# Layer 1's vertical 5-tap convolution: two rows at a time from eight products in place of ten

## The chip, the cores and the metric

The kernel runs on one core of a Trainium2 chip. The metric is device time in microseconds (us) for the whole kernel, the median of several runs; smaller is better. The kernel before takes 4054.06 us (three runs, 4048.38 to 4065.66).

## What is computed

Two layers work on an image tensor `x` of shape (2, 128, 256, 256): two images, 128 channels, 256 rows of 256 columns, all in float32. Layer 0 is an attention over windows of 8x8 pixels; the change does not touch it. Layer 1 is cut here to what matters:

```python
def _L1_conv_ref(x, w1, w3, w4):                    # x: after a group norm
    t1 = conv(x, w1, padding=((2, 2), (0, 0)))      # 5 taps along the rows, 128 -> 128 channels
    t3 = conv(t1, w3, padding=((1, 1), (0, 0)),     # 3 taps along the rows, each channel by itself
              feature_group_count=c)
    t2 = _unfold_w3_dil2(x)                         # columns w-2, w, w+2
    t4 = einsum('nckhw,ckg->nghw', t2, w4)          # 128 channels -> 8 groups
    t5 = t4[:, None] * t3.reshape(n, c // g, g, h, w)
    return t5.reshape(n, c, h, w)
...
x = x + _L1_conv_ref(_gn(x), w1, w3, w4)
```

With channels on the 128 partitions, each tap of `w1` is one 128x128 matrix that multiplies rows of `x`. Two rows of 256 columns are 512 elements, which fill one bank of the accumulator memory (PSUM). So a pair of output rows costs five products of a 128x128 matrix with 128x512 elements.

## The kernel before: the part of layer 1

The kernel walks through each image in 32 strips of 8 rows, so there are 64 strips in all. `xt` holds the 12 normalised rows that a strip needs, with two such buffers in turn. `t1` holds 10 rows: rows 0 and 1 are taken over from the strip before, rows 2 to 9 are new.

```python
rawp  = tile_pool("f_raw1", bufs=4); tp = tile_pool("f_t1", bufs=2); wk = tile_pool("f_wk1", bufs=2)
ps_pj = tile_pool("f_ps_pj1", bufs=1, space=PSUM)
ps_a  = tile_pool("f_ps_a", bufs=2, space=PSUM)     # 2 banks for the vertical convolution
ps_g  = tile_pool("f_ps_g", bufs=1, space=PSUM)
ps_b  = tile_pool("f_ps_b", bufs=1, space=PSUM)     # 4 tags, 4 banks
# ... cut: weights; xn = two buffers of [P, 12, 260] ...

def normalise1(b, s, k, mean, rstd):
    cur, prev = xn[k % 2], xn[(k + 1) % 2]
    # ... cut: the first strip of an image ...
        nc.gpsimd.tensor_copy(cur[:, 0:4, :], prev[:, 8:12, :])                       # L528
    n = 8 if s + 1 < NS else 5
    nc.vector.tensor_scalar(                                                          # L530
        cur[:, 4 : 4 + n, 2 : 2 + W], raws[b, s][:, 0:n, :], mean, rstd, ALU.subtract, ALU.mult)
    # ... cut ...

for k in range(NB * NS):
    b, s = divmod(k, NS)
    xt = xn[k % 2]
    t1 = tp.tile([P, 10, W], F32, tag="t1", name=f"t1_{k}")
    # ... cut: row 1 of the first strip of an image, three products over one row ...
        nc.gpsimd.tensor_copy(t1[:, 0:2, :], t1s[k - 1][:, 8:10, :])                  # L562
    # ... cut ...
    for j in (2, 4, 6, 8):
        n = 1 if j == 8 and s + 1 == NS else 2
        pa = ps_a.tile([P, 512], F32, tag="a", name=f"a_{k}_{j}")
        for tap in range(5):
            nc.tensor.matmul(                                                         # L570
                pa[:, : n * W], w1[:, tap, :], xt[:, j - 2 + tap : j - 2 + tap + n, 2 : 2 + W],
                start=tap == 0, stop=tap == 4)
        nc.scalar.copy(t1[:, j : j + n, :].rearrange("p r w -> p (r w)"), pa[:, : n * W])   # L574
    pg = ps_g.tile([P, 512], F32, tag="g", name=f"g_{k}")
    for tap in range(3):
        for j in range(4):
            nc.tensor.matmul(                                                         # L579
                pg[32 * j : 32 * j + 32, :], w4[:, tap, :],
                xt[:, 2 * j + 1 : 2 * j + 3, 2 * tap : 2 * tap + W], start=tap == 0, stop=tap == 2)
    t4 = wk.tile([P, 512], F32, tag="t4", name=f"t4_{k}")
    nc.scalar.copy(t4, pg)                                                            # L585
    t3 = wk.tile([P, 8, W], F32, tag="t3", name=f"t3_{k}")
    nc.scalar.activation(t3, t1[:, 0:8, :], AF.Copy, scale=w3[:, 0:1])                # L587
    for tap in (1, 2):
        nc.vector.scalar_tensor_tensor(                                               # L589
            t3, t1[:, tap : tap + 8, :], w3[:, tap : tap + 1], t3, ALU.mult, ALU.add)
    y = wk.tile([P, 8, W], F32, tag="y", name=f"y_{k}")
    for j in range(4):
        pb = ps_b.tile([P, 512], F32, tag=f"b{j}", name=f"b_{k}_{j}")
        nc.tensor.matmul(pb, sel[32 * j : 32 * j + 32, :], t4[32 * j : 32 * j + 32, :],
                         start=True, stop=True)                                       # L596
        nc.vector.tensor_tensor(y[...rows 2j, 2j+1...], pb, t3[...the same rows...], ALU.mult)   # L599
    nc.gpsimd.tensor_tensor(y[:, 0:3, :], y[:, 0:3, :], raws[b, s - 1][:, 5:8, :], ALU.add)   # L603
    nc.gpsimd.tensor_tensor(y[:, 3:8, :], y[:, 3:8, :], raws[b, s][:, 0:5, :], ALU.add)       # L604
    nc.gpsimd.dma_start(out[b, :, 8 * s : 8 * s + 8, :], y)                           # L605
    if k + 1 < NB * NS:
        start_strip(k + 1)        # loads rows, then normalise1
```

The order in which each engine gets its instructions isn't the order of this text: a scheduler ahead of the run sets it, from what it takes to be ready, and work of neighbouring strips is interleaved. On the chip each engine then follows its own list in that order.

Of the kernel before, what the change touches and what calls it, by code (L numbers as in the profile page):

```python
# [9 lines left out]
F32 = mybir.dt.float32  # L10
I32 = mybir.dt.int32
AF = mybir.ActivationFunctionType
ALU = mybir.AluOpType
# [5 lines left out]
P = 128  # L19
W = 256  # L20
# [458 lines left out]
def convolutions_fast(tc, io, x1_d, norm, st_y, out):  # L479

    nc = tc.nc
    NB, _, H, _ = io["x"].shape
    NS = H // 8
    with ExitStack() as l1:
        cst = l1.enter_context(tc.tile_pool(name="f_l1c", bufs=1))
        rawp = l1.enter_context(tc.tile_pool(name="f_raw1", bufs=4))
        tp = l1.enter_context(tc.tile_pool(name="f_t1", bufs=2))
        wk = l1.enter_context(tc.tile_pool(name="f_wk1", bufs=2))
        ps_pj = l1.enter_context(tc.tile_pool(name="f_ps_pj1", bufs=1, space=PSUM))
        ps_a = l1.enter_context(tc.tile_pool(name="f_ps_a", bufs=2, space=PSUM))  # L490
        ps_g = l1.enter_context(tc.tile_pool(name="f_ps_g", bufs=1, space=PSUM))
        ps_b = l1.enter_context(tc.tile_pool(name="f_ps_b", bufs=1, space=PSUM))

        w1 = cst.tile([P, 5, P], F32, tag="w1", name="w1")
        nc.sync.dma_start(w1, io["w1T"])
        w3 = cst.tile([P, 3], F32, tag="w3", name="w3")
        nc.sync.dma_start(w3, io["w3"])
        w4 = cst.tile([P, 3, 32], F32, tag="w4", name="w4")
        nc.sync.dma_start(w4, io["w4g"])
        sel = cst.tile([P, P], F32, tag="sel", name="sel")  # L500
        nc.sync.dma_start(sel, io["c_sel"])
        xn = [cst.tile([P, 12, 260], F32, tag=f"xm{i}", name=f"xm{i}") for i in range(2)]
        for i in range(2):
            nc.gpsimd.memset(xn[i], 0.0)

        raws = {}

        def load_rows1(b, s):

            if s == 0:  # L510
                pre = rawp.tile([P, 8, W], F32, tag="raw", name=f"raw1_{b}_pre")
                nc.sync.dma_start(pre[:, 5:8, :], x1_d[b][0][:, 0:3, :])
                raws[b, -1] = pre
            t = rawp.tile([P, 8, W], F32, tag="raw", name=f"raw1_{b}_{s}")
            nc.sync.dma_start(t[:, 0:5, :], x1_d[b][s][:, 3:8, :])
            if s + 1 < NS:
                nc.sync.dma_start(t[:, 5:8, :], x1_d[b][s + 1][:, 0:3, :])
            raws[b, s] = t

        def normalise1(b, s, k, mean, rstd):  # L520
            cur, prev = xn[k % 2], xn[(k + 1) % 2]
            if s == 0:
                nc.gpsimd.memset(cur[:, 0:1, :], 0.0)
                nc.vector.tensor_scalar(
                    cur[:, 1:4, 2 : 2 + W], raws[b, -1][:, 5:8, :], mean, rstd, ALU.subtract, ALU.mult
                )
            else:
# [3 lines that stand above are left out]
                cur[:, 4 : 4 + n, 2 : 2 + W], raws[b, s][:, 0:n, :], mean, rstd, ALU.subtract, ALU.mult  # L531
            )
            if n < 8:
                nc.gpsimd.memset(cur[:, 4 + n : 12, :], 0.0)

        norms = {}
        t1s = {}

        def start_strip(k):
            b, s = divmod(k, NS)  # L540
            if s == 0:
                norms[b] = norm.group(st_y[b], ps_pj, f"y{b}")
            load_rows1(b, s)
            normalise1(b, s, k, *norms[b])

        start_strip(0)
# [5 lines that stand above are left out]
            if s == 0:  # L552
                nc.gpsimd.memset(t1[:, 0:1, :], 0.0)
                pa = ps_a.tile([P, 512], F32, tag="a", name=f"a_{k}_first")
                for tap in (2, 3, 4):
                    nc.tensor.matmul(
                        pa[:, 0:W], w1[:, tap, :], xt[:, tap - 1, 2 : 2 + W],
                        start=tap == 2, stop=tap == 4,
                    )
                nc.scalar.copy(t1[:, 1, :], pa[:, 0:W])  # L560
            else:
                nc.gpsimd.tensor_copy(t1[:, 0:2, :], t1s[k - 1][:, 8:10, :])  # L562
            t1s[k] = t1
            if s + 1 == NS:
                nc.gpsimd.memset(t1[:, 9:10, :], 0.0)  # L565
            for j in (2, 4, 6, 8):
                n = 1 if j == 8 and s + 1 == NS else 2
                pa = ps_a.tile([P, 512], F32, tag="a", name=f"a_{k}_{j}")
                for tap in range(5):
                    nc.tensor.matmul(  # L570
                        pa[:, : n * W], w1[:, tap, :], xt[:, j - 2 + tap : j - 2 + tap + n, 2 : 2 + W],
                        start=tap == 0, stop=tap == 4,
                    )
                nc.scalar.copy(t1[:, j : j + n, :].rearrange("p r w -> p (r w)"), pa[:, : n * W])  # L574

            pg = ps_g.tile([P, 512], F32, tag="g", name=f"g_{k}")
            for tap in range(3):
# [3 lines that stand above are left out]
                        xt[:, 2 * j + 1 : 2 * j + 3, 2 * tap : 2 * tap + W],  # L581
                        start=tap == 0, stop=tap == 2,
# [7 lines that stand above are left out]
                    t3, t1[:, tap : tap + 8, :], w3[:, tap : tap + 1], t3, ALU.mult, ALU.add  # L590
# [6 lines that stand above are left out]
                    pb, sel[32 * j : 32 * j + 32, :], t4[32 * j : 32 * j + 32, :], start=True, stop=True  # L597
                )
                nc.vector.tensor_tensor(  # L599
                    y[:, 2 * j : 2 * j + 2, :].rearrange("p r w -> p (r w)"), pb,  # L600
                    t3[:, 2 * j : 2 * j + 2, :].rearrange("p r w -> p (r w)"), ALU.mult,
# [4 lines that stand above are left out]
            del raws[b, s - 1]  # L606
            if k + 1 < NB * NS:
                start_strip(k + 1)
# [592 lines left out]
```

## Time and profile before

| what | value |
|---|---|
| time, median of 3 runs | 4054.06 us |
| span of the profiled execution | 4070.9 us |
| TensorE matmuls, busy | 3641.6 us, 89% |
| VectorE, busy | 2272.4 us, 56% |
| ScalarE, busy | 1384.2 us, 34% |
| GpSimd, busy | 1084.9 us, 27% |
| last product of attention's stage begins | 2663.28 us |
| first products of layer 1 (`a_first`) begin | 2678.85 us |
| last products of layer 1 (`b`) begin | 4046.72 us |

In the profile's words PE is TensorE, DVE is VectorE, ACT is ScalarE, POOL is GpSimd; PEld is the loading of weights, which runs beside the matmuls. A group of instructions is named by its line in the kernel (the marks `L570` and so on in the code above), its engine, and what it writes and reads. "Busy" is the union of the instructions' durations; the mean of one matmul is longer than the pace at which matmuls follow each other, since they are pipelined. One float32 product in the program shows as two matmul instructions in the trace.

### The profile page before, as it was taken

What the parts mean: (1) busy time and instruction counts of PE and PEld (TensorE: products, weight loads), DVE (VectorE), ACT (ScalarE), POOL (GpSimd) and SP (SyncE); (2) the same over time, 40 slices, a digit from 0 to 9 for tenths busy, and PEclk for the clock granted to TensorE, in tenths of its full rate; (3) what the DMA queues carried; (4) which work ended last, traced back from release to release, by engine and by line L of the source; (5) the groups of instructions that cost most, each with busy time, mean ns of one, the idle gap of its engine ahead of it and who ended that gap; (6) DMA issues with size and microseconds to landing.
All of it is one profiled execution on the core that took longest, in us unless ns stands there. A gap on an engine that the chain in (4) does not pass through costs nothing. (4 is left out here: it accounts for less than half of the span.)

```text
span 4070.9 us, 144840 instructions
## 1 busy us (share of the span) xinstructions
PE 3641.6 (89%) x67638; PEld 2218.5 (54%) x67638; DVE 2272.4 (56%) x3377; ACT 1384.2 (34%) x2237; POOL 1084.9 (27%) x914
## 2 busy tenths in 40 slices
PE   0778988889989888988988989989999999999997
PEld 0556666666666666666666666643333334333333
DVE  8777656565655565656556565544444444444443
ACT  0333444444444444444444444422222222222221
POOL 1212222122222222212222122123333333333333
PEclk9999999999999999999999999989999999999998
DMA  9562212212212121221212211122222222222221
GB/s 377 190 198 81 68 60 68 68 55 68 72 56 65 55 68 55 73 68 55 68 55 73 68 55 65 34 92 104 97 90 104 104 93 96 101 103 104 90 97 70
DMA packets 71315, 362.10 MB, mean 89 GB/s; under 512 B 8496, under 2 KB 9136, under 8 KB 50224
## 3 DMA queue, kind: packets, MB, share of 16 engines
q1 hardware_dynamic: 43056, 218.49, 16.3%
q0 software_dynamic: 27648, 134.23, 8.4%
q8 instruction: 533, 8.73, 0.9%
q14 instruction: 78, 0.64, 0.1%
HBM read 218.48 MB, written 134.22 MB: 87 GB/s over the span
## 5 line engine op out<-in xcount | busy, mean ns | idle before, releaser
L570 PE MATMUL a<-xm,w 128*128 128x512 f32 (+1 forms) x2560 | 1129.8, 594 | 0.0
L570 PEld LDWEIGHTS a<-xm,w 128*128 128x128 f32 x2560 | 471.6, 188 | 654.5 <-issue 653.8
L589 DVE SCALAR_TENSOR_TENSOR t<-t,w,t 128x2048 f32<-128x2048 f32 x128 | 323.2, 2525 | 752.7 <-ACT t L574 752.6
L348 DVE COPY f_vt<-f_pv 64x512 f32<-64x512 f32 x512 | 354.1, 694 | 656.1 <-ACT f_vt L348 653.6
L348 ACT COPY f_vt<-f_pv 64x512 f32<-64x512 f32 x512 | 298.5, 583 | 756.2 <-PE f_pv L341 756.2
L341 PE MATMUL f_pv<-f_wqkvT,f_xn 128*64 128x128 f32 x8192 | 521.0, 286 | 29.6 <-issue 29.2
L374 PEld LDWEIGHTS f_s<-f_q,f_kt 32*64 32x64 f32 x32768 | 405.0, 134 | 194.0 <-issue 185.4
L374 PE MATMUL f_s<-f_q,f_kt 32*64 32x32 f32 x32768 | 411.6, 227 | 106.9 <-issue 106.6
L341 PEld LDWEIGHTS f_pv<-f_wqkvT,f_xn 128*64 128x64 f32 x8192 | 482.3, 144 | 43.1 <-issue 36.4
L574 ACT COPY t<-a 128x512 f32<-128x512 f32 (+1 forms) x256 | 149.6, 585 | 901.7 <-PE a L570 886.4
L268 POOL COPY f_xq<-f_xn 128x512 f32<-128x512 f32 x256 | 350.8, 1407 | 330.3 <-DVE f_xn L260 295.4
L321 ACT ACTIVATE f_cf<-f_pa,f_keep 128x256 f32<-128x256 f32 x256 | 207.1, 809 | 535.2 <-PE f_pa L315 534.5
L425 DVE TENSOR_TENSOR f_x<-f_py,f_raw 128x512 f32<-128x512 f32 x256 | 176.9, 693 | 263.3 <-PE f_py L424 260.7
L382 ACT ACTIVATE f_p<-f_s 128x512 f32<-128x512 f32 x512 | 265.4, 602 | 131.8 <-PE f_s L374 131.8
L286 POOL COPY f_kt<-f_kt 128x524 f32<-128x524 f32 x124 | 83.0, 669 | 841.5 <-ACT f_kt L281 841.5
L395 PEld LDWEIGHTS f_o<-f_vt,f_p 128*32 128x32 f32 x16384 | 241.4, 110 | 107.5 <-ACT f_kt L281 77.4
L315 PE MATMUL f_pa<-f_xq,f_wb 128*128 128x128 f32 x2048 | 276.5, 286 | 17.8 <-DVE f_on L402 14.6
L278 PE MATMUL f_pk<-f_xn,f_wqkvT 128*128 128x512 f32 (+1 forms) x528 | 277.0, 647 | 15.6 <-DVE f_vt L348 10.5
L395 PE MATMUL f_o<-f_vt,f_p 128*32 128x66 f32 x16384 | 263.6, 222 | 9.0 <-DVE f_x L425 9.0
L315 PEld LDWEIGHTS f_pa<-f_xq,f_wb 128*128 128x128 f32 x2048 | 248.7, 192 | 33.8 <-issue 14.7
L253 POOL COPY f_xn<-f_xn 128x1048 f32<-128x1048 f32 x62 | 71.1, 1146 | 732.2 <-PE f_pv L341 732.2
L424 PE MATMUL f_py<-f_ot,f_woT 128*128 128x512 f32 x512 | 246.3, 603 | 4.0 <-DVE f_ot L409 2.5
(103 smaller groups left out, 3601.4 us busy)
## 6 DMA issues: line engine op xcount, KB each, us to landing
f_raw<-in_x SPq DMA_DIRECT2D x62, 1280.0 KB, 7.0
f_x<-f_x POOLq DMA_DIRECT2D x128, 512.0 KB, 5.0
out<-y POOLq DMA_DIRECT2D x64, 1024.0 KB, 4.5
raw<-f_x SPq DMA_DIRECT2D x64, 640.0 KB, 4.2
f_sx<-in_x SPq DMA_DIRECT2D x32, 1024.0 KB, 12.4
f_sx<-in_x SPq DMA_DIRECT2D x64, 512.0 KB, 3.9
raw<-f_x SPq DMA_DIRECT2D x62, 384.0 KB, 4.7
f_raw<-in_x SPq DMA_DIRECT2D x2, 1024.0 KB, 5.6
```

What stands on the lines that cost most here:

```text
L268: nc.gpsimd.tensor_copy(xq[:, t2], by_place[:, t2])
L278: nc.tensor.matmul(pk[:, : n * P], wkT, xt[:, r, c, 1:129, lo:hi], start=True, stop=True)
L315: nc.tensor.matmul(pa[:, P * t1 : P * t1 + P], wb[:, t2, t1].rearrange("p h x -> p (h x)"), xq[:, t2, t1].rearrange("p a m -> p (a m)"), s ...
L321: nc.scalar.activation(cf[:, 0, t2], by_e[:, 0], AF.Identity, bias=keep[:, 1:2], scale=keep[:, 0:1])
L341: nc.tensor.matmul(pv[64 * c : 64 * c + 64, P * n : P * n + P], xt[:, r, c, o : o + 64], wvT, start=True, stop=True,)
L348: (nc.vector.tensor_copy if c else nc.scalar.copy)(vt[rows, 4 * j : 4 * j + 4, :, c, 0:32], pv[rows].rearrange("p (n h d) -> p n h d", n=4 ...
L374: nc.tensor.matmul(sc[h][64 * c : 64 * c + 64, 32 * n : 32 * n + 32], keys_k[rows, c, 48 * n : 48 * n + 64], qs[u][rows, c, 32 * n : 32 * ...
L382: nc.scalar.activation(pts[u][:, h], sc[h], AF.Exp)
L395: nc.tensor.matmul(po[32 * h : 32 * h + 32, n - lo], p[:, h, 32 * n : 32 * n + 32], vt[:, n, h], start=True, stop=True,)
L424: nc.tensor.matmul(py, woT, ots.pop((u, c)), start=True, stop=True)
L570: nc.tensor.matmul(pa[:, : n * W], w1[:, tap, :], xt[:, j - 2 + tap : j - 2 + tap + n, 2 : 2 + W], start=tap == 0, stop=tap == 4,)
L589: nc.vector.scalar_tensor_tensor(t3, t1[:, tap : tap + 8, :], w3[:, tap : tap + 1], t3, ALU.mult, ALU.add)
```

## The change

An odd and an even output row share their inputs. Write the five taps as `w0..w4`, and split rows and taps by parity. With `P0` the even taps on even rows, `P1` the odd taps on odd rows, and `P2` the sums of neighbouring taps on the sums of neighbouring rows, the even output row is `P0 + P1` of the row pair before, and the odd one is `P2 - P0 - P1`. `P0` takes three products, `P1` two and `P2` three: eight in place of ten for two rows, over two pairs at a time (512 columns) sixteen in place of twenty for a strip. The change is there to take products from TensorE. In return it needs sums of rows of the input (`sm`), sums of weights (`w1s`, once), and additions and subtractions of the three parts.

```diff
+        w1s = cst.tile([P, 2, P], F32, tag="w1s", name="w1s")
+        nc.vector.tensor_add(w1s[:, 0], w1[:, 4], w1[:, 3])
+        nc.vector.tensor_add(w1s[:, 1], w1[:, 2], w1[:, 1])
 ...
-            for j in (2, 4, 6, 8):
-                n = 1 if j == 8 and s + 1 == NS else 2
-                pa = ps_a.tile([P, 512], F32, tag="a", name=f"a_{k}_{j}")
-                for tap in range(5):
-                    nc.tensor.matmul(... five taps ...)
-                nc.scalar.copy(t1[:, j : j + n, :].rearrange("p r w -> p (r w)"), pa[:, : n * W])
+            sm = tp.tile([P, 6, W], F32, tag="sm", name=f"sm_{k}")
+            lo = 0 if s == 0 else 2
+            nc.gpsimd.tensor_tensor(
+                sm[:, lo:6], xt[:, 2 * lo : 12 : 2, 2 : 2 + W], xt[:, 2 * lo + 1 : 12 : 2, 2 : 2 + W],
+                ALU.add,
+            )
+            if s > 0:
+                nc.gpsimd.tensor_copy(sm[:, 0:2], sms[k - 1][:, 4:6])
+            sms[k] = sm
+            p0 = wk.tile([P, 4, W], F32, tag="p0", name=f"p0_{k}")
+            p1 = tp.tile([P, 5, W], F32, tag="p1", name=f"p1_{k}")
+
+            def taps(name, out, n, terms):
+                pa = ps_a.tile([P, 512], F32, tag="a", name=f"a_{k}_{name}")
+                for i, (w, rows) in enumerate(terms):
+                    nc.tensor.matmul(
+                        pa[:, : n * W], w, rows, start=i == 0, stop=i == len(terms) - 1
+                    )
+                if out is not None:
+                    nc.scalar.copy(out.rearrange("p r w -> p (r w)"), pa[:, : n * W])
+                return pa
+
+            def rows(j, n=2):
+                return xt[:, j : j + 2 * n - 1 : 2, 2 : 2 + W]
+
+            if s == 0:
+                taps("p1", p1[:, 0:1], 1, [(w1[:, 3], rows(3, 1)), (w1[:, 1], rows(1, 1))])
+            for m in (2, 4):
+                taps(
+                    f"p0_{m}", p0[:, m - 2 : m], 2,
+                    [(w1[:, 4 - 2 * i], rows(2 * m - 2 * i)) for i in range(3)],
+                )
+                taps(
+                    f"p1_{m}", p1[:, m - 1 : m + 1], 2,
+                    [(w1[:, 3 - 2 * i], rows(2 * m + 1 - 2 * i)) for i in range(2)],
+                )
+            nc.gpsimd.tensor_tensor(
+                t1[:, 2, :], p0[:, 0], p1[:, 0] if s == 0 else p1s[k - 1][:, 4], ALU.add
+            )
+            nc.gpsimd.tensor_tensor(t1[:, 4:9:2, :], p0[:, 1:4], p1[:, 1:4], ALU.add)
+            p1s[k] = p1
+            for m in (2, 4):
+                n = 1 if m == 4 and s + 1 == NS else 2
+                pa = taps(
+                    f"p2_{m}", None, 2,
+                    [(w, sm[:, m - i : m - i + 2]) for i, w in enumerate((w1s[:, 0], w1s[:, 1], w1[:, 0]))],
+                )
+                odd = t1[:, 2 * m - 1 : 2 * m + 2 * n - 2 : 2, :]
+                nc.vector.tensor_tensor(
+                    odd, pa[:, : n * W].rearrange("p (r w) -> p r w", w=W), p0[:, m - 2 : m - 2 + n],
+                    ALU.subtract,
+                )
+                nc.vector.tensor_tensor(odd, odd, p1[:, m - 1 : m - 1 + n], ALU.subtract)
```

## The prediction

> **What bounds the kernel now.** I looked first at the page's busy times. TensorE's 89% stands for two stages, so I cut the span where layer 1 begins (its first products start at 2678.85 us) and where its last products start (4046.72 us), and asked for the busy time of the engines in that stretch and in one strip.
>
> ```profile
> 2678.80:4046.70 1367.90, 1367.16 (x4612) 537.30 (x4612) 597.49 (x445) 315.82 (x386) 466.65 (x319) 1.00 0.27 96
> 3217.89:3239.25 21.36, 21.36 (x76) 8.36 (x72) 9.45 (x8) 4.93 (x6) 7.40 (x5) 1.00 0.27 98
> ```
>
> The columns are the stretch, its length, then busy us of PE, PEld, DVE, ACT and POOL, the granted clock and the DMA. Layer 1 is 1367.9 us, 64 strips of 21.36 us, with TensorE busy for all of it; VectorE has 9.45 us of work in a strip, ScalarE 4.93, GpSimd 7.40. But pipelined matmuls can look busy while they wait, so I took TensorE's own timeline to see whether it keeps a pace.
>
> ```profile
> 3239.26 16.58 PE L570 MATMUL a<-xm,w 128*128 128x512 f32 x38
> 3255.77 2.79 PE L579 MATMUL g<-xm,w 128*32 128x512 f32 x24
> 3258.49 1.13 PE L570 MATMUL a<-xm,w 128*128 128x512 f32 x2
> 3259.55 1.14 PE L596 MATMUL b<-t,sel 32*128 32x512 f32 x8
> 3260.61 1.55 PE L570 MATMUL a<-xm,w 128*128 128x512 f32 x3
> ```
>
> There is no hole. A strip is 40 instructions of the vertical convolution (38 and 2 of the next strip), the 24 of `g` (2.72 us from start to start) and the 8 of `b` (1.06). Weight loads within the vertical convolution start 0.43 us apart all through the strip (3203.08, 3203.51, 3203.94, ...; ten of them from 3203.08 to 3207.38 are 4.30 us apart), so an instruction costs 0.429 us and a product, two instructions, 0.858. Twenty products are 17.2 us of the 21.36. TensorE bounds layer 1.
>
> Next the costs on the other engines, from the groups by line and shape over four strips (busy us, mean ns of one, then idle time before and who ended it):
>
> ```profile
> L589 DVE SCALAR_TENSOR_TENSOR t<-t,w,t 128x2048 f32<-128x2048 f32 x8 | 19.9, 2481 | 47.6 <-ACT t L574 47.6
> L604 POOL TENSOR_TENSOR y<-y,raw 128x1280 f32<-128x1280 f32 x4 | 11.6, 2889 | 0.0
> ...
> L574 ACT COPY t<-a 128x512 f32<-128x512 f32 x16 | 9.4, 586 | 56.6 <-PE a L570 56.6
> L530 DVE TENSOR_SCALAR xm<-raw,mean_y,rstd_y 128x2048 f32<-128x2048 f32 x4 | 8.3, 2072 | 0.0
> L587 ACT ACTIVATE t<-t,w 128x2048 f32<-128x2048 f32 x4 | 8.0, 2002 | 0.3
> L603 POOL TENSOR_TENSOR y<-y,raw 128x768 f32<-128x768 f32 x4 | 7.2, 1809 | 19.2 <-DVE y L599 19.2
> ```
>
> Everything waits for TensorE. Last, the timelines of VectorE and of GpSimd over one strip, because the change loads just these two:
>
> ```profile
> 3235.20 2.72 DVE L589 SCALAR_TENSOR_TENSOR t<-t,w,t 128x2048 f32<-128x2048 f32 x1 [11.82 <-ACT t L574]
> 3237.84 2.07 DVE L530 TENSOR_SCALAR xm<-raw,mean_y,rstd_y 128x2048 f32<-128x2048 f32 x1
> 3239.83 2.33 DVE L589 SCALAR_TENSOR_TENSOR t<-t,w,t 128x2048 f32<-128x2048 f32 x1
> 3242.26 2.48 DVE L599 TENSOR_TENSOR y<-b,t 128x512 f32<-128x512 f32 x4
> ```
>
> ```profile
> 3235.17 0.60 POOL L562 COPY t<-t 128x512 f32<-128x512 f32 x1 [7.38 <-ACT t L574]
> 3237.25 1.58 POOL L528 COPY xm<-xm 128x1040 f32<-128x1040 f32 x1 [1.48 <-PE g L579]
> ```
>
> The two engines get in each other's way. L528 starts at 3237.25 and the L589 beside it ends at 3237.92; then L528 needs 0.91 us, to 3238.83; then L530, begun at 3237.84, needs 1.07, to 3239.91. At the first strips the same sums come out: two L530 without GpSimd beside them take 2.60 us together, and there L528 ends 0.90 us after them. So L528 alone is 0.91 us, L530 alone about 1.1 to 1.3, and the rest of their durations is waiting for each other. L589 is 2.33 alone.
>
> **What the Trainium skill says.** "SBUF — State Buffer", section "SBUF: two separate sides", says that VectorE and GpSimd share one port pair to SBUF as an exclusive lock: a VectorE operation in a 2-port mode, or with two SBUF inputs against a GpSimd operation that reads SBUF, and a GpSimd operation shut each other out for whole instructions. The three durations above agree with that to 0.02 us. "VectorE: DVE Perf Modes", section "Mode 2×_2P — use both read ports for one tensor", has the one-input float32 operation at two elements a cycle by that second port, and no `tensor_tensor` so: L530's 1.07 us for 2048 elements against L589's 2.33 agrees. "GPSIMD Engine Reference", section "3.1 Elementwise — side-by-side cycle accounting", gives 4497 ns for a two-input addition of 2048 float32, an estimate of 2.2 ns an element; L604 and L603 differ by 512 elements and 1.08 us, 2.11 ns an element. "FP8 and Floating Point Precision", section "TensorE Precision Notes", has true FP32 as four passes; the trace shows two instructions for each product, and the passes inside them it doesn't show.
>
> **The change part by part.**
>
> TensorE. An ordinary strip has 3+2+3+2 products for `p0` and `p1` and 3+3 for `p2`, 16 in place of 20. The row step of two in the moving operand leaves runs of 256 elements, so I keep 0.858 us. That is 3.43 us a strip: 21.36 becomes 17.93. The last strip of an image had 17.5 (five of one row's width) and gets 16; the first gets two more of one row, one product's worth. In all 62 x 4 + 2 x 1.5 - 2 x 1 = 249 products, 213.6 us, all on the path.
>
> ScalarE. Four evictions of 128x512 before and four after (0.59 each); `p2` isn't evicted. 4.93 us stay.
>
> VectorE. Two subtractions for each `p2`, four of 512 elements. L599 has the same form (one operand from PSUM) and four of it take 2.48 us. So 2.5 us more: 9.45 to about 12 of 17.93.
>
> GpSimd. The row sums, 1024 elements: 1.81 + 256 x 2.11 ns = 2.35 us. The copy of two sum rows, as L562: 0.60. The even rows: 256 elements, 1.81 - 512 x 2.11 ns = 0.73, and 768 elements, 1.81. In all 5.49: 7.40 to 12.9.
>
> No engine alone comes to 17.93. The shared port does. Before, a strip holds it for L604 2.89, L603 1.81, L528 0.91, L562 0.60, L589 2 x 2.33, L530 1.07: 11.9 of 21.36. The change adds GpSimd's 5.49 and the second subtraction of each pair, both of whose operands are in SBUF, 2 x 0.62: 18.7 us. If the fixed part of each instruction doesn't hold the lock (some 0.1 us of thirteen), 17.4. It is level with TensorE. So I don't expect the whole gain: I expect GpSimd and VectorE to lag until the lag reaches TensorE now and then, and put a strip at 18.4, half a microsecond above TensorE's own work.
>
> Tail. Before, L587 (2.0 us) ran ahead of the last eviction, since it reads rows 0 to 7. Now row 7 comes from the last `p2`, through two subtractions. At the end of the kernel this adds 2 x 0.62 + 2.0 - 0.36, about 3 us.
>
> Sum: 4054 - 213.6 + 3 = 3843 if TensorE alone sets the pace; plus 64 x 0.5 = 32: **3875 us**.
>
> **The rivals.**
>
> 1. TensorE keeps its pace throughout (17.93, 3843 us). For it: what TensorE waits for has slack. The `p2` banks are freed by the first subtraction; bank 1 has a `p2` and `g` to spare (2.57 + 2.72 us), bank 2 `g`, `b` and three products (6.4). `sm` can be made a strip ahead. Against it: the port's 18.7.
>
> 2. The list of GpSimd ties strip to strip. If it holds the additions of `y` (k) ahead of the even rows of k+1, the loop is L587 2.0, L530 1.07, L589 4.66, L599 2.48, L604 2.89, even rows 2.54, about 16.2 with the hand-overs; it fits. With `sm` and its copy (2.95) in between it is 19.2 us a strip, 64 x 1.27 more: about 3924.
>
> 3. ScalarE holds back `b`. L587 becomes ready in the middle of `g`; if it goes ahead of the eviction of `g` (L585), `b` comes up to 1.6 us late, and TensorE, with one product listed ahead of `b`, would wait. At most 64 x 1.6: 3945. A scheduler that lists two or three products there takes it away.
>
> 4. PSUM. Six tiles go through the two banks in a strip in place of four, and the shortest filling of the other bank is 1.72 us. An eviction is 0.59, so it is hidden unless ScalarE stands in L587. I give it little.
>
> **Range and chances.** The floor is 3843, and only a faster product would go below; 3835 is the low end. Rivals 2 and 3 in full end at 3924 and 3945, so 3950 is the high end. A gain under 2% would need 19.9 us a strip or more (3973), that is two of the rivals at once; slower would need more than 22.6, for which nothing in the sums speaks. Faster by over 2%: 0.92, within: 0.06, slower: 0.02.
>
> **What would show it.** In the profile after, a strip of 17.9 to 18.9 us; products still 0.43 us apart for an instruction; GpSimd's row sums near 2.4 us and VectorE's second subtractions lengthened beyond 0.62 by lock waits; GpSimd and VectorE with few common idle times. I'd be wrong in the sum if the strip comes out at 17.93 (the port has room after all), and wrong in kind if TensorE stands idle for 2 us or more in each strip, or if strided rows slow the products.

## The result and the profile after

The changed kernel takes 3920.89 us (four runs, 3910.18 to 3933.43) against 4053.02 us before (four runs): a ratio of 0.967, 95% interval 0.9627 to 0.9714. That is 132 us less. The prediction was 3875 us, 178 less, with a range of 3835 to 3950.

Where layer 1 begins in the span differs by some 40 us between executions in which nothing ahead of it was changed (2646.97 to 2688.64 us over all profiles here), so layer 1 is measured from its own first products (`a_first`) to its own last products (`b`): 1367.9 us before (2678.85 to 4046.72), 1237.0 us after (2646.97 to 3883.95). The gain of 130.9 us is the whole gain, and three fifths of what TensorE was freed of.

The busy times of two strips of the changed kernel (columns as before: stretch, its length, PE, PEld, DVE, ACT, POOL):

```profile
2746.40:2765.60 19.20, 18.00 (x64) 6.87 (x64) 16.79 (x13) 4.40 (x6) 16.77 (x9) 1.00 0.30 109
...
3207.06:3226.21 19.15, 17.99 (x65) 6.84 (x65) 17.00 (x13) 4.82 (x6) 17.39 (x11) 1.00 0.24 89
```

A strip takes 19.2 us in the mean (24 strips from 2746.40 to 3207.06), not 21.36. TensorE works for 17.99 of them, as foreseen, but it is no longer busy all the time. VectorE shows 17 us in place of 9.45, GpSimd 17 in place of 7.40. TensorE's timeline says where it stands still:

```profile
3220.35 2.79 PE L630 MATMUL g<-xm,w 128*32 128x512 f32 x24
3223.07 1.98 PE L588 MATMUL a_p<-xm,w 128*128 128x512 f32 x4
3226.21 1.14 PE L647 MATMUL b<-t,sel 32*128 32x512 f32 x8 [1.16 <-ACT t L636]
```

In each strip it has one hole, ahead of `b`, and it waits there for the eviction of `g` (L636, before L585). From strip to strip the hole is 0.7 to 1.7 us, 1.2 in the mean: 17.99 + 1.2 is the strip. The chain that leads to this `b` (start, us, what):

```profile
3221.55 2.05 DVE t L625
...
3223.72 1.87 issue
3225.59 0.57 ACT t L636
3226.16 0.04 issue
3226.21 1.14 PE b L647 x8
```

Read upward, `b` waits for the eviction of `g`; ScalarE can't begin that until it is done with the first tap (L638, before L587; it begins at 3223.68 and its 2.0 us are the "issue" of 1.87 here); the first tap waits for the second subtraction (L625) of the second `p2`. And L625 takes 2 us, where the first subtraction L621 of as many elements takes 0.69. The groups from 2720 to 3200 us show it as a mean:

```profile
L640 DVE SCALAR_TENSOR_TENSOR t<-t,w,t 128x2048 f32<-128x2048 f32 x50 | 170.4, 3409 | 8.7 <-ACT t L638 7.9
L575 POOL TENSOR_TENSOR sm<-xm 128x1024 f32<-128x1024 f32 x25 | 109.9, 4398 | 18.7 <-DVE xm L534 18.7
L625 DVE TENSOR_TENSOR t<-t,p 128x512 f32<-128x512 f32 x51 | 103.8, 2035 | 5.7 <-DVE t L621 0.5
...
L609 POOL TENSOR_TENSOR t<-p,p 128x256 f32<-128x256 f32 x25 | 69.4, 2775 | 0.0
...
L534 DVE TENSOR_SCALAR xm<-raw,mean_y,rstd_y 128x2048 f32<-128x2048 f32 x25 | 60.8, 2432 | 1.3 <-PE g L630 0.6
```

These are the operations that share the port: the taps (3.41 us, alone 2.33), the row sums (4.40, alone 2.36), the second subtraction (2.04), one even row (2.78, alone 0.72), the normalisation (2.43, alone 1.35). Each shows longer than it is alone. That this is waiting for the other engine at the port is shown by an experiment for the second subtraction below; for the others it is read from where the other engine's operations end.

### The profile page after: what moved, and what is told of

It reads as the page before. It is cut to its first block, busy times and chain, and to the rows that moved or that the text cites. A ratio compares the mean times of both kernels' runs of the same rounds, so it can differ in the third digit from the quotient of the medians.

```text
span 3908.4 us, 144671 instructions
## 1 busy us (share of the span) xinstructions
PE 3431.7 (88%) x67134; PEld 2125.0 (54%) x67134; DVE 2734.8 (70%) x3635; ACT 1377.4 (35%) x2239; POOL 1674.5 (43%) x1168
## 4 chain that ended last, share of the span: by engine, by line
PE 64%; DVE 22%; issue 9%; DMA 3%; ACT 1%; POOL 1%; DVEq 0%; ACTq 0%; POOLq 0%; SPq 0%
PE a_p L588 17%; PE f_pv L341 12%; PE f_s L374 9%; PE f_pk L278 6%; PE f_py L424 5%; DVE t L625 5%; PE f_s L360 3%; PE f_pa L315 3%; PE f_o L395 3%; PE f_pq L297 3%; DVE f_on L402 2%; DMA f_sx<-in_x 2%; DVE st_y L109 2%; DVE f_cf L324 2%; DVE f_ot L409 2%
## 5 line engine op out<-in xcount | busy, mean ns | idle before, releaser
L588 PE MATMUL a_p<-xm,w 128*128 128x512 f32 (+1 forms) x1288 | 588.2, 602 | 0.0
L640 DVE SCALAR_TENSOR_TENSOR t<-t,w,t 128x2048 f32<-128x2048 f32 x128 | 429.3, 3354 | 30.4 <-ACT t L638 28.1
L588 PEld LDWEIGHTS a_p<-xm,w 128*128 128x128 f32 x1288 | 234.1, 189 | 349.7 <-issue 337.2
L638 ACT ACTIVATE t<-t,w 128x2048 f32<-128x2048 f32 x64 | 128.1, 2002 | 497.5 <-DVE t L625 497.5
L592 ACT COPY p<-a_p 128x512 f32<-128x512 f32 (+1 forms) x258 | 150.5, 583 | 423.3 <-PE a_p L588 423.3
L575 POOL TENSOR_TENSOR sm<-xm 128x1024 f32<-128x1024 f32 (+1 forms) x64 | 271.4, 4241 | 49.9 <-DVE xm L534 49.9
```

The lines of the kernel that those rows point to most:

```text
L575: nc.gpsimd.tensor_tensor(sm[:, lo:6], xt[:, 2 * lo : 12 : 2, 2 : 2 + W], xt[:, 2 * lo + 1 : 12 : 2, 2 : 2 + W], ALU.add,)
L588: nc.tensor.matmul(pa[:, : n * W], w, rows, start=i == 0, stop=i == len(terms) - 1)
L640: nc.vector.scalar_tensor_tensor(t3, t1[:, tap : tap + 8, :], w3[:, tap : tap + 1], t3, ALU.mult, ALU.add)
```

## The experiments

A strip is given below as the mean from one `b` to the next over 21 to 26 strips of the same image; it sees only layer 1. A ratio is to the kernel before on the same chip. Four theories were put up against each other, the first three before the first run:

1. Order: `b` waits because ScalarE's list has the late first tap ahead of the eviction of `g`.
2. Capacity: VectorE and GpSimd can't do a strip's work at the shared port in less than about 19 us.
3. Lock: the first tap is late because the second subtractions wait at the port.
4. Loop (after the first four runs): the first tap of a strip hangs, through GpSimd's list, on the first tap of the strip before.

**The changed kernel again,** on the chip of the next three runs.

> The changed kernel once more, as the neighbour of the other runs. Every theory: about 3921 us, a strip of 19.2 us in the middle of an image, TensorE waiting about 1.2 us a strip ahead of b.

3940.60 us, ratio 0.9684 (0.9613 to 0.9755), a strip of 19.20 us.

**The order on ScalarE.**

```diff
-            nc.scalar.copy(t4, pg)
+            ev = nc.scalar.copy(t4, pg)
...
-            nc.scalar.activation(t3, t1[:, 0:8, :], AF.Copy, scale=w3[:, 0:1])
+            with tc.issue_after(ev.ins):
+                nc.scalar.activation(t3, t1[:, 0:8, :], AF.Copy, scale=w3[:, 0:1])
```

The edit also let the scheduler list `b` one product earlier on TensorE, as in the kernel before.

> ScalarE's list has the eviction of g ahead of the first tap (t3) in every strip; nothing else is changed in what is computed. Theory 1 (order: b waits only because the eviction of g stands behind a late t3): the wait ahead of b goes, the strip becomes 18.0 us, 64 x 1.2 = 77 us less than the changed kernel, about 3845 us. Theory 2 (the shared port is full, and VectorE and GpSimd cannot do a strip's work in less than about 19 us): the wait moves to where b's banks or p2's banks come free, the strip stays at 18.7 us or more, time 3890 us or more. VectorE's second subtraction stays near 2.0 us in both.

3939.20 us, ratio 0.9665 (0.9598 to 0.9733), a strip of 19.16 us: nothing gained. The hole ahead of `b` is gone, and there is another one. TensorE, then ScalarE, of that kernel:

```profile
3028.19 1.14 PE L648 MATMUL b<-t,sel 32*128 32x512 f32 x8
3029.26 3.70 PE L588 MATMUL a_p<-xm,w 128*128 128x512 f32 x8
3034.47 4.56 PE L588 MATMUL a_p<-xm,w 128*128 128x512 f32 x10 [1.51 <-ACT p L592]
```

```profile
3031.94 2.00 ACT L639 ACTIVATE t<-t,w 128x2048 f32<-128x2048 f32 x1 [4.00 <-DVE t L625]
3033.85 1.05 ACT L592 COPY p<-a_p 128x512 f32<-128x512 f32 x2
```

The eviction of `g` is done by 3027.94, and the first tap comes at 3031.94, 4.00 us after it, and the evictions of the next strip's `p0` and `p1` (L592) stand behind it, so TensorE waits for a bank. Theory 1 falls: `b` was only where the lateness came to light. The second subtractions didn't stay near 2.0 us, as had been expected; their mean is 2.80. Something makes the first tap come every 19.2 us, whatever ScalarE does first.

**The second subtraction reads from PSUM.**

```diff
-                nc.vector.tensor_tensor(odd, pa[...], p0[:, m - 2 : m - 2 + n], ALU.subtract)
-                nc.vector.tensor_tensor(odd, odd, p1[:, m - 1 : m - 1 + n], ALU.subtract)
+                part = pa[:, : n * W].rearrange("p (r w) -> p r w", w=W)
+                nc.vector.tensor_tensor(part, part, p0[:, m - 2 : m - 2 + n], ALU.subtract)
+                nc.vector.tensor_tensor(odd, part, p1[:, m - 1 : m - 1 + n], ALU.subtract)
```

> The lists of all engines as in the changed kernel; the first subtraction writes back into PSUM, so that the second has one operand there and not two in SBUF. Theory 3 (lock: t3 is late because the second subtractions wait for GpSimd at the port): they fall from 2.0 us to about 0.7, t3 is ready some 2.5 us sooner, the wait ahead of b is gone or under 0.2 us a strip although the order stays bad, time about 3845 to 3855 us. If the second subtraction is slow by itself (a fixed cost, not the lock), it stays at 2.0 us and the time stays at 3921 us. Theory 2 (port full): the port is relieved by only 1.2 us a strip, so the strip falls to 18.5 us at best in the mean, 3875 us or more.

3904.37 us, ratio 0.9581 (0.9513 to 0.9649), a strip of 18.66 us. All engines have the lists of the changed kernel. The second subtraction (now L623) falls from 2.04 to 0.69 us (mean over the stretch from 2720 to 3200 us):

```profile
L623 DVE TENSOR_TENSOR t<-a_p,p 128x512 f32<-128x512 f32 x52 | 35.9, 691 | 1.8
```

So its length was the lock and not its own; but the strip loses just 0.54 us. Theory 3 is right on what made the subtraction long and wrong on the size of the gain. By itself this run fits what theory 2 expected (18.5 us at best). What the first tap (now L636) waits for has changed. ScalarE, GpSimd and VectorE of that kernel over one strip:

```profile
3007.45 2.00 ACT L636 ACTIVATE t<-t,w 128x2048 f32<-128x2048 f32 x1 [7.31 <-POOL t L612]
...
3026.11 2.00 ACT L636 ACTIVATE t<-t,w 128x2048 f32<-128x2048 f32 x1 [7.30 <-POOL t L612]
```

```profile
3008.45 1.05 POOL L532 COPY xm<-xm 128x1040 f32<-128x1040 f32 x1
3010.67 4.41 POOL L575 TENSOR_TENSOR sm<-xm 128x1024 f32<-128x1024 f32 x1 [1.17 <-DVE xm L534]
3015.03 2.78 POOL L609 TENSOR_TENSOR t<-p,p 128x256 f32<-128x256 f32 x1
3018.68 1.81 POOL L652 TENSOR_TENSOR y<-y,raw 128x768 f32<-128x768 f32 x1 [0.87 <-DVE y L648]
3020.45 2.89 POOL L653 TENSOR_TENSOR y<-y,raw 128x1280 f32<-128x1280 f32 x1
3023.64 0.55 POOL L654 DMA_DIRECT2D out<-y  x1 [0.30 <-POOL y L653]
3024.22 1.86 POOL L612 TENSOR_TENSOR t<-p,p 128x768 f32<-128x768 f32 x1
```

```profile
3007.54 3.05 DVE L534 TENSOR_SCALAR xm<-raw,mean_y,rstd_y 128x2048 f32<-128x2048 f32 x1 [1.33 <-PE g L628]
3010.51 6.72 DVE L638 SCALAR_TENSOR_TENSOR t<-t,w,t 128x2048 f32<-128x2048 f32 x2
3017.32 2.48 DVE L648 TENSOR_TENSOR y<-b,t 128x512 f32<-128x512 f32 x4
```

Follow it from 3007.45: first tap; VectorE comes to the taps at 3010.51, since L534 has waited for GpSimd's copies (three in a row, L532 is the last); the taps take 6.72 us with the row sums between them; two products `y` are ready and L652 starts at 3018.68; L653, the issue of the output and then the even rows of the next strip (L612), which had their inputs by 3018.80 (the last eviction begins at 3018.22) and stood in the list behind; and at 3026.11 the next first tap. 3.06 + 6.81 + 1.36 + 1.77 + 3.19 + 0.58 + 1.89 = 18.66 us. Steps between one first tap and the next must add up to a strip; what makes them a loop is that each begins when the one before it lets it (the first tap and the copies that hold L534 back both begin when L612 is done). None of these steps is TensorE's work, but L534 has waited for TensorE too (1.33 us, for `g`); whether it would go ahead of the copies if `g` came earlier, this run doesn't show. In the changed kernel the same loop goes one step further: there the last subtraction, 3221.55 to 3223.59, waits at the port for L612, which ends at 3223.03 and adds the half microsecond to 19.2:

```profile
3221.17 1.86 POOL L612 TENSOR_TENSOR t<-p,p 128x768 f32<-128x768 f32 x1
```

In other strips of that kernel it lets a copy go first as well; strips of 19.7 and 18.7 us often alternate there, and 19.2 is their mean. That gave theory 4.

**Both edits together.**

> Both edits. Theories 1 and 3: the two mend the same wait, so together they bring no more than one alone, about 3843 us, the pace of TensorE's own work. Theory 2: better than each alone, since both ease the port's queue, and still above 3860 us.

3949.42 us, ratio 0.9707 (0.9638 to 0.9776), a strip of 19.20 us (the first three of the image at 17.9, then 18.7 or 19.6). None of the theories expected a loss against the second edit alone. In the waits TensorE stands 19.4 us over 18 strips for the evictions of `p0` behind the first tap, as with the first edit. In two strips of three L534 begins before the copies, and then the first of the two taps (L639) waits while GpSimd goes through L532, L575 and L609 without a pause:

```profile
3029.33 1.04 POOL L532 COPY xm<-xm 128x1040 f32<-128x1040 f32 x1
3030.34 2.34 POOL L575 TENSOR_TENSOR sm<-xm 128x1024 f32<-128x1024 f32 x1
3032.65 0.72 POOL L609 TENSOR_TENSOR t<-p,p 128x256 f32<-128x256 f32 x1
```

```profile
3029.29 8.62 DVE L639 SCALAR_TENSOR_TENSOR t<-t,w,t 128x2048 f32<-128x2048 f32 x2 [0.93 <-ACT t L637]
```

The taps take 8.62 us there in place of 6.72, and from the first tap to the products `y` it is 10.75 us (3027.25 to 3038.00), where it was 9.87 with the second edit alone. That is the 0.9 us by which the loop is longer in these strips. Why L534 comes first there stays open.

**The loop cut in GpSimd's list.** On top of the subtraction in PSUM, the additions of `y` and the output of a strip are written down after the next strip's even rows and queued behind them:

```diff
-            nc.gpsimd.tensor_tensor(t1[:, 4:9:2, :], p0[:, 1:4], p1[:, 1:4], ALU.add)
+            ev = nc.gpsimd.tensor_tensor(t1[:, 4:9:2, :], p0[:, 1:4], p1[:, 1:4], ALU.add)
+            if ends:
+                with tc.issue_after(ev.ins):
+                    ends.pop()()          # y additions and output of the strip before
```

> The kernel with the subtraction in PSUM (e2_psum), and in GpSimd's list the even rows of a strip now stand ahead of the additions of y of the strip before; work, engines and the port's load are the same as in e2_psum, which had a strip of 18.66 us. Theory 4 (loop by the list: t3 waits for the even rows, these stand behind y of the strip before, which waits for that strip's t3): the loop is cut, t3 waits for VectorE alone, no wait ahead of b, a strip of 18.0 us, some 43 us less than e2_psum, ratio to the kernel before about 0.948. Theory 2 (the port's capacity): the same load, so the strip stays at 18.6 to 18.7 us, ratio 0.958.

3855.77 us, ratio 0.951 (0.9474 to 0.9545), a strip of 17.93 us. TensorE has no hole left, with the same instructions on the same engines as in the kernel of 18.66 us. That shows theory 4 and refutes theory 2 for this load, 17.4 us at the port by the prediction's costs. The changed kernel's own load is 1.24 us more, with its second subtractions at the port. TensorE, then GpSimd:

```profile
3030.35 1.99 PE L589 MATMUL a_p<-xm,w 128*128 128x512 f32 x4
3032.27 1.14 PE L649 MATMUL b<-t,sel 32*128 32x512 f32 x8
```

```profile
3023.24 1.81 POOL L613 TENSOR_TENSOR t<-p,p 128x768 f32<-128x768 f32 x1
3025.02 1.80 POOL L657 TENSOR_TENSOR y<-y,raw 128x768 f32<-128x768 f32 x1
3026.79 2.92 POOL L658 TENSOR_TENSOR y<-y,raw 128x1280 f32<-128x1280 f32 x1
```

Layer 1 takes 1156.2 us here (2668.88 to 3825.06); the sum for TensorE alone had been 1367.9 - 213.6 = 1154.3.

**The copies on ScalarE.** Again on top of the subtraction in PSUM, with GpSimd's list otherwise unchanged:

```diff
-                nc.gpsimd.tensor_copy(cur[:, 0:4, :], prev[:, 8:12, :])
+                nc.scalar.copy(cur[:, 0:4, :], prev[:, 8:12, :])
...  the same for t1[:, 0:2] and sm[:, 0:2]
```

> e2_psum with the three copies of rows (xm, t1, sm) on ScalarE in place of GpSimd, GpSimd's other work in the same order. Both theories 2 and 4 expect a gain, since the loop loses VectorE's wait for those copies (about 1.9 us) and the port loses 2.1 us: a strip of 18.0 us, ratio about 0.948. If ScalarE's copies get ahead of t3 or of the eviction of g, a wait ahead of b of some tenths of a us stays.

3854.49 us, ratio 0.9509 (0.9472 to 0.9547), a strip of 17.92 us. L534 falls from 3.03 to 1.35 us, which takes 1.7 us out of a loop of 18.66 and so leaves it under TensorE's 17.93. The list is the bad one, but the loop is short enough. The copies also leave the port (2.1 us less of load), so this run alone doesn't tell loop from load; the one with the cut loop does. These two are the fastest of all, with ratios of 0.951 where the changed kernel has 0.967.

**More load at the port.** The kernel with the cut loop does one addition of row sums more in each strip, which nothing reads:

```diff
+            more = wk.tile([P, 4, W], F32, tag="more", name=f"more_{k}")
+            nc.gpsimd.tensor_tensor(more, xt[:, 4:12:2, 2 : 2 + W], xt[:, 5:12:2, 2 : 2 + W], ALU.add)
```

> e8_even_first with one more addition of row sums on GpSimd in each strip, whose result nothing reads (1024 elements, 2.35 us). Summed up, the port is then held 17.4 + 2.35 = 19.8 us a strip. Theory 2 (the port is a bound of its own as soon as its sum passes TensorE's 18.0): a strip of 19.3 to 20 us. Theory 4 alone (only the order hurts, the sum overstates the port): a strip under 18.6 us.

3969.38 us, ratio 0.9792 (0.9745 to 0.9839), a strip of 20.08 us: 2.15 us more for a load of 2.35, where theory 2 expected 19.3 to 20. So the capacity is real: 20.08 - 2.35 = 17.73 us is an estimate of what the kernel with the cut loop needs, just under TensorE's 17.93. Whether the port is full or GpSimd's own list, with its waits, these runs don't tell apart. GpSimd's timeline in part:

```profile
3007.09 4.39 POOL L576 TENSOR_TENSOR sm<-xm 128x1024 f32<-128x1024 f32 x1 [1.18 <-DVE xm L534]
3011.45 4.44 POOL L584 TENSOR_TENSOR more<-xm 128x1024 f32<-128x1024 f32 x1
```

GpSimd's whole list runs without a pause but for 1.18 us behind L534 and 0.30 ahead of the output; each of the two additions carries one tap's length of waiting (4.4 us, of which 2.36 are its own). In the kernel with the cut loop, the pauses are these two and 0.13 us ahead of L613: GpSimd was full there too, and it came out even with TensorE.

**The same load where no chain leads to TensorE.** The kernel before, with two such additions in each strip:

> The kernel before with two additions of row sums on GpSimd in each strip, whose results nothing reads (4.7 us more at the port, 16.6 of 21.36 us in sum). No chain to TensorE is touched, so theories 2 and 4 both expect a strip of 21.36 us and the time of the kernel before within 0.5%, with the two taps on VectorE (2.33 us alone) lengthened where an addition stands in their way. A strip over 21.6 us would mean that load on the port hurts by itself, well below its sum.

4060.15 us against 4057.35, ratio 1.0005 (0.9985 to 1.0024), a strip of 21.36 us. One addition shows as 4.40 us with a tap in its way and the other as 2.36 us without. Where no chain leads from it to TensorE, this waiting at the port costs nothing.

**Each cure alone on the changed kernel,** with both subtractions as the change has them: only GpSimd's list, and only the copies.

> The changed kernel with only GpSimd's list changed (even rows ahead of the additions of y of the strip before); both subtractions as in the changed kernel, the second with two operands in SBUF. If the list's loop alone made the excess, the strip falls from 19.2 to 18.0 us. If the second subtractions' waits at the port are the other half, they stay near 2 us, t3 is late by them, and the strip stays between 18.4 and 19.2 us. Ratio 0.950 against 0.957 to 0.967.

3919.78 us, ratio 0.9655 (0.9628 to 0.9682), a strip of 19.00 us. The loop is cut, and now the subtractions stand in the way inside the strip: the even rows come first, the additions of `y` behind them hold the port just when VectorE subtracts. The last subtraction (3023.61 to 3025.72) ends 0.55 us after L660 (3021.79 to 3025.17), and the first tap, the eviction of `g` and `b` follow it; TensorE waits 1.01 us ahead of `b`.

> The changed kernel with only the three copies of rows moved to ScalarE. The loop by GpSimd's list loses VectorE's wait for these copies (some 1.9 us), so theory 4 expects about 18.0 us a strip if nothing but that loop counts; with the second subtractions still waiting at the port for the additions of y, 18.2 to 18.7 us. Ratio 0.950 to 0.960. If only the second subtractions count and the loop doesn't, 19.2 us as in the changed kernel.

3886.63 us, ratio 0.9553 (0.9519 to 0.9586), a strip of 18.43 us. The loop is shorter, the second subtractions are still long (1.46 us).

Against 19.19 us for the changed kernel, one edit alone gave 19.00 (list), 18.66 (PSUM) and 18.43 (copies); PSUM with either of the others gave TensorE's own 17.93. The remaining pair, list and copies, was not run.

## Why the prediction was right, and where it was off

**TensorE's part** held: 17.99 us of matmuls in a strip for a predicted 17.93, strided rows and all, and 1156.2 us of layer 1 where nothing else holds it for a predicted 1154.3.

**The costs of the new instructions** held where they ran alone: row sums 2.36 us (2.35 predicted), one even row 0.72 to 0.73 (0.73), three even rows 1.81 (1.81), subtractions 0.69 against 0.62. L530 was read too low: the 1.07 us is only what was left of it after L528, alone it takes 1.35 (L534 in the runs with the copies on ScalarE). So its agreement with the lock "to 0.02 us" came in part from taking that rest for the whole. ScalarE stayed at 4.8 us a strip. "Second subtractions lengthened beyond 0.62 by lock waits" came as said, at 2.04.

**The step that was too small** is "put a strip at 18.4, half a microsecond above TensorE's own work". It was 19.2, 1.26 above, and outside the 17.9 to 18.9 us given as the sign of being right. 0.8 us in 64 strips is 51 us, and the prediction was 46 off. The lag didn't reach TensorE "now and then" either, but in every strip. The half microsecond had no working of its own: it stood for the port's sum of 17.4 to 18.7 against 17.93. But that sum is only what the port must carry, not when. The run with the cut loop carried 1.24 us less than the changed kernel in 17.93 us; no run carried the changed kernel's whole load at that pace, and with only the list changed it took 19.00.

**The missing piece was named** as the second rival, and it gave "19.2 us a strip" with `sm` between. I took it as a rival to be weighed, where it should have been the reckoning, since most of it was in view: the row sums that get in between the taps, and the additions of `y` ahead of the next even rows. These links are in the trace of the subtraction in PSUM, with 18.66 us. Its total of 19.2 fits the changed kernel partly by luck: it had no half microsecond for the second subtraction, was somewhat high on the rest, and put L587 and L530 in a row (2.0 + 1.07 us) where the run has L534 waiting for three copies beside the first tap, 3.06 us in all.

**The third rival**, ScalarE, is what the waits show as TensorE's hole (1.2 us of the 1.6 allowed). The run that turned ScalarE's order round shows that this order alone wasn't the cause.

**The first rival** (no loss at all) failed as the change stands and came true with two edits. **The fourth** (banks) does not show in the changed kernel; TensorE waited for evictions only where ScalarE's order was turned round.

**The end.** From the start of the last `b` to the issue of the last output it is 10.65 us after and 8.62 before: 2.0 us more there, for about 3 predicted. Not foreseen: at the change of image, where the first tap is late by more, TensorE waits once for 5.6 us.

## What to carry to other kernels

When work is taken from the engine that bounds a kernel and sums are put on VectorE and GpSimd in return, adding up each engine's time isn't enough, and nor is the sum at the port they share. Write down what the next strip's first result waits for through each engine's list, go once around, and compare that loop with the pace you hope for. If the loop is longer, cut it where old work stands ahead of new work in a list, or shorten it, as here by moving copies from GpSimd to ScalarE. The load still counts: one addition more on GpSimd cost nearly its whole length. The wait that the profile shows on the bounding engine may be just where the loop touches it; turning the order round at that place moved the wait and gained nothing.

## What was new in the behaviour of the hardware

- A VectorE operation that waits for GpSimd at the port ends about 0.55 us after GpSimd's operation, for 512 elements: 3023.59 after 3023.03 in the changed kernel, 3025.72 after 3025.17 in the run with the list alone. That is a little less than the 0.69 us of the whole instruction, so some of its own time, 0.14 us, lies in the wait. In the prediction I asked whether fixed parts hold the port; this says that not all of an instruction does.
- Where both engines had work waiting, they often took turns by instruction: two taps in a row had the row sums between them, and row sums and an even row each waited for a tap (4.40 for 2.36 us, 2.78 for 0.73). A short operation then pays for a long one: one even row of 0.73 us took 2.78. But it is no rule. With both edits a tap that began at 3029.29 waited for three GpSimd operations in a row, to 3033.37, and with the subtraction in PSUM L534 (3.05 us, alone 1.35) waited for three copies.
- With one of its two operands in PSUM, the second subtraction showed no wait for GpSimd: it stayed at 0.69 us beside GpSimd's additions.
